# Two outlook-attention layers: the first pair's statistics pass keeps its transposed blocks in SBUF, and its stores, zero fills and output weights move into the first columns of the loop

## The chip, the cores and the metric

The kernel runs on one core of one Trainium2 chip. A core has five engines with instruction streams of their own: TensorE (PE; its weight loads are listed as PEld), VectorE (DVE), ScalarE (ACT), GpSimd (POOL) and SyncE (SP), and 16 DMA engines. Here SP and ACT issue all transfers that the kernel asks for, each on a queue of its own. The metric is the device time of one execution in microseconds, given as the median over several runs.

## The reference

The input x is 8 images of 56 x 56 positions with 384 channels, in float32. Two layers follow one another, each of the form x + f(groupnorm(x)). Group norm takes mean and variance over a whole image for each of 32 groups of 12 channels, so nothing of an image can be normalized before all of it was seen.

```python
# layer 0 (heads 12, 32 channels each), g = groupnorm(x)
v    = g @ Wv.T                                   # values, then 3x3 patches of them, zero outside
a    = softmax((g @ Wa.T).reshape(b, n, 12, 9, 9) * 32**-0.5)   # 9x9 weights per position and head
out  = einsum('bnhpq,bnqhd->bnphd', a, patches(v))
y    = overlap_add(out)                           # each of 9 results goes to its own neighbour
x    = x + y @ Wo.T
# layer 1 (heads 6, 64 channels each), g = groupnorm(x)
a    = softmax((g @ W_attn + b_attn).reshape(b, n, 6, 9))       # 9 weights per position and head
v    = g @ W_v + b_v
x    = x + einsum('bpKhd,bphK->bphd', patches(v), a) @ W_proj + b_proj
```

## The kernel before, in words

**Tiling.** The images are worked in 4 pairs. The two images of a pair lie above one another: R = 112 rows, 56 columns. The layer 0 loop goes over columns, one step for each column of each pair (4 x 56 steps and 3 more). Eight groups of 7 columns (`px`) of a pair are the patches in which attention weights meet values. All matmuls have the channels or the positions on the partitions, 128 or 112 of them.

**The opening.** Before the loop the kernel computes the group-norm statistics of pair 0, alone. It reads x in 14 blocks of 4 columns (`stats_load`, 672 KB each, into `xr`, two buffers), turns each block with 12 TensorE transposes into `xt` (channels on partitions, two buffers; three chunks of 128 channels, `stats_chunk`), copied out of PSUM by ACT, and feeds DVE's `bn_stats` from it. When a block is whole, SP stores it to the DRAM tensor `xT` (line 413). `norm_params` then adds up the statistics, spreads them over the groups by small matmuls with the matrix `gmat` (`over_groups`: for each of two quantities three output chunks of 128 channels, each summed over three input chunks) and makes scale and bias. Other work at the head of SP's and POOL's streams: loads of the weights `wv` and `wo`, zero fills of DRAM tables (`clears`, `fill`), zeroing of the two large SBUF buffers `zs` (line 455), the first of which also holds the raw weights `wa` before they are rearranged.

**The loop.** In step c `attend` projects column c of the normalized `xn` on the attention weights (lines 119, 486, 487), ACT takes exp (491), DVE sums and inverts, POOL scales (510). It also projects values (`bank<-wv_t`), which ACT copies and stores to the table `vtab0` (line 296, ACT's queue). `presum` for column c-2 adds neighbouring weights on POOL (529 to 533), and `fold` for column c-3 shifts them by a small matmul (`pw`), the result of which goes to the tables `ztab0` (line 561, ACT's queue). `upkeep` does what has to be done beside it: statistics of the next pair (loads on ACT's queue, one chunk a step), clearing, `load` of an `xT` block into `xin` (two buffers, ACT's queue, line 460), and `normed`, which turns `xin` into `xn`, with 8 columns in two halves. At column 10 of a group of seven `fetch_v` has SP read the patches of `vtab0`, one step later `fetch` has it read those of `ztab0` into the two `zs`, and the residual `xres` from `xT`. The contraction (`pc`) and the output projection (`po`, with `wo`) of the patch are queued as jobs with the due time step + 4 and are run two a step between the matmuls of the following columns.

**What sets the order.** A planner orders each engine's instructions. It starts what is ready, by its own estimate, and prefers what comes earlier in the program, so that a load can stand far ahead of its place in the code. A buffer of a pool goes to the next tile when every user of the former tile is through. `tc.keep_in_program_order` pins an instruction behind the instruction that precedes it in the program on the same engine. All matmuls and transposes and all zero fills are pinned. [...]

**Layer 1** follows with the same columns and patches, other tables and a matrix for values and weights together; the change doesn't touch it, but for `norm_params`, which makes its scale and bias too.

Of the kernel before, what the change touches and what calls it, by code (L numbers as in the profile page):

```python
# [8 lines left out]
F32 = mybir.dt.float32  # L9
# [6 lines left out]
def two_outlook_layers(  # L16
# [32 lines left out]
    nc = tc.nc  # L49

    B, H, W, C = x.shape
    P = 128
    NCH = C // P
    IMG = 2
    R = IMG * H
# [65 lines left out]
    def transpose(*args, **kwargs):  # L121
        tc.keep_in_program_order(nc.tensor.transpose(*args, **kwargs))  # L122


    ident = const.tile([P, P], F32, name="ident")
    make_identity(nc, ident)
# [49 lines left out]
    def fill(table, first, dims, width):  # L176

        src = zeros[: dims[0][1], :width]
        if len(dims) > 1:
            src = src.unsqueeze(1).to_broadcast([dims[0][1], dims[1][1], width])  # L180
        tc.keep_in_program_order(
            nc.sync.dma_start(bass.AP(table.tensor, table.offset + first, [*dims, [1, width]]), src)
        )

    def clear_v(table, sx, pad):

        line = sx * C
        part = line // 12
        fill(table, 0, [[(R + GAP) * line, NPX + 1], [part, 12 * GAP]], part)
        fill(table, GAP * line, [[line, R], [C, pad]], C)  # L190
        fill(
            table, ((NPX - 1) * (R + GAP) + GAP) * line + (sx - pad) * C,
            [[line, R], [C, pad]], C,
        )

    def clear_weights(table, line, part, sx, slot, row, first, e, ep):
        fill(table, 0, [[part, MARGIN * line // part]], part)
        fill(table, (MARGIN + R) * line, [[part, (MARGIN + 1) * line // part]], part)
        top = MARGIN * line
        fill(table, top, [[line, R]], first * row)  # L200
        fill(table, top + (first + e) * row, [[line, R], [slot, sx]], (ep - e) * row)

    def clears():

        yield 0, lambda: clear_v(vtab0, SX0, 2)

        yield 0, lambda: fill(
            ztab0[0], MARGIN * LINE0 + FIRST0 * ROW0, [[LINE0, R], [SLOT0, 2]], E0 * ROW0
        )
        for n, t in enumerate(ztab0):  # L210
            yield (1, 2 * PX, 3 * PX)[n], lambda t=t: clear_weights(
                t, LINE0, 366, SX0, SLOT0, ROW0, FIRST0, E0, EP0
            )
        yield 4 * PX, lambda: clear_v(vtab1, SX1, 1)
        for n, t in enumerate(ztab1):
            yield (5 + n) * PX, lambda t=t: clear_weights(
                t, LINE1, 350, SX1, SLOT1, ROW1, FIRST1, K, EP1
            )
# [6 lines left out]
    eps_t = const.tile([P, 1], F32, name="eps_t")  # L225
    nc.gpsimd.memset(eps_t, EPS)

    def weight(pool, src, n, name):
        t = pool.tile([P, NCH, n], F32, name=name)
        nc.sync.dma_start(t, src.rearrange("(i p) n -> p i n", p=P))  # L230
        return t

    def norm_params(st, name, params, key):

        mv = stat.tile([P, NCH, IMG, 2], F32, tag="mv", name=f"mv_{name}")

        def over_groups(src, what):
            pg = ps.tile([P, NCH, IMG], F32, tag="t", name=f"p{what}_{name}")
            for j in range(NCH):
                for i in range(NCH):  # L240
                    matmul(
                        pg[:, j, :], gmat[:, i, j * P : (j + 1) * P], src[:, i, :],
                        start=(i == 0), stop=(i == NCH - 1),
                    )
            g = stat.tile([P, NCH, IMG], F32, tag=what, name=f"{what}_{name}")
            nc.vector.tensor_copy(g, pg)
            return g

        for i in range(NCH):
            for b in range(IMG):  # L250
                nc.vector.bn_aggr(mv[:, i, b, :], st[:, i, b, :, :])
        yield
        mean = over_groups(mv[:, :, :, 0], "gmean")

        part = stat.tile([P, NCH, IMG], F32, tag="part", name=f"part_{name}")
        nc.vector.tensor_sub(part, mv[:, :, :, 0], mean)
        nc.vector.tensor_mul(part, part, part)
        nc.vector.tensor_add(part, part, mv[:, :, :, 1])
        yield
        var = over_groups(part, "gvar")  # L260
        std = stat.tile([P, NCH, IMG], F32, tag="std", name=f"std_{name}")
        nc.scalar.activation(std, var, AF.Sqrt, bias=eps_t)
        scale = const.tile([P, NCH, IMG], F32, name=f"scale_{name}")
        nc.vector.reciprocal(scale, std)
        bias = const.tile([P, NCH, IMG], F32, name=f"bias_{name}")
        nc.vector.scalar_tensor_tensor(bias, mean, -1.0, scale, ALU.mult, ALU.mult)
        params[key] = scale, bias
        yield
# [49 lines left out]
    class Jobs:  # L318


        def __init__(self):
            self.queue = []
# [30 lines left out]
    def patch_tiles(name, b):  # L353
        return patch.tile([P, NPY0, C], F32, tag="vp", name=f"vp_{name}_{b}")
# [25 lines left out]
    def layer0(late, pools):  # L380
# [5 lines left out]

        stats, st1s, params, xins, attns, pres, xrs, xts = {}, {}, {}, {}, {}, {}, {}, {}

        def stats_load(pair, blk, queue):
            nm = f"{pair}_{blk}"  # L390
            xr = io.tile([P, XB, C], F32, tag="xr", name=f"xr_{nm}")[:R]
            queue.dma_start(xr, xf[pair * R : (pair + 1) * R, blk * XB : (blk + 1) * XB, :])
            xrs[pair, blk] = xr

        def stats_chunk(pair, blk, i, alone):

            nm = f"{pair}_{blk}"
            if blk == 0 and i == 0:
                stats[pair] = stat.tile([P, NCH, IMG, NBLK, 6], F32, tag="st0", name=f"st0_{pair}")
            if i == 0:  # L400
                xts[pair, blk] = io.tile([P, NCH, XB, R], F32, tag="xt", name=f"xt_{nm}")
            xr, xt = xrs[pair, blk], xts[pair, blk]
            if alone:
                pt = bank(P, 0, XB * R).rearrange("p (m r) -> p m r", m=XB)
            else:
                pt = ps.tile([P, XB, R], F32, tag="t", name=f"pt_{nm}_{i}")
            for j in range(XB):
                transpose(pt[:, j, :], xr[:, j, i * P : (i + 1) * P], ident[:R, :R])
            nc.scalar.copy(xt[:, i], pt)
            for b in range(IMG):  # L410
                nc.vector.bn_stats(stats[pair][:, i, b, blk, :], xt[:, i, :, b * H : (b + 1) * H])
            if i == NCH - 1:
                nc.sync.dma_start(
                    xTs[pair][:, :, blk * XB * R : (blk + 1) * XB * R], xt.rearrange("p i m r -> p i (m r)")
                )
                del xrs[pair, blk], xts[pair, blk]

        stats_load(0, 0, nc.sync)
        for blk in range(NBLK):
            if blk + 1 < NBLK:  # L420
                stats_load(0, blk + 1, nc.sync)
            for i in range(NCH):
                stats_chunk(0, blk, i, True)
        for _ in norm_params(stats.pop(0), "0_0", params, 0):
            pass

# [22 lines left out]
                )  # L449
        for t in banks:  # L450
            nc.vector.memset(t[:, BANK - NP0 + NL :], 0.0)
        wv_t = weight(fixed, wv0, C, "wv0_t")
        wo_t = weight(late_w, wo0, C, "wo0_t")
        for z in zs:
            nc.gpsimd.memset(z, 0.0)

        def load(g):
            pair, blk = divmod(g, NBLK)
            xins[g] = io.tile([P, NCH, XB, R], F32, tag="xin", name=f"xin_{g}")
            nc.scalar.dma_start(  # L460
                xins[g].rearrange("p i m r -> p i (m r)"),
                xTs[pair][:, :, blk * XB * R : (blk + 1) * XB * R],
            )
# [187 lines left out]
        def upkeep(step):  # L651

            pair, c = divmod(step, W)
            while clearing and clearing[0][0] <= step:
                clearing.pop(0)[1]()
            if pair + 1 < NPAIR:
                blk, i = divmod(c - 3, NCH)
                if 0 <= c and i == 0 and blk < NBLK - 1:
                    stats_load(pair + 1, blk + 1, nc.scalar)
                if 3 <= c and blk < NBLK:  # L660
                    stats_chunk(pair + 1, blk, i, False)
                elif NBLK * NCH + 3 <= c < NBLK * NCH + 6:
                    if c == NBLK * NCH + 3:
                        making["0"] = norm_params(stats.pop(pair + 1), f"0_{pair + 1}", params, pair + 1)
                    next(making["0"])
            g, j = divmod(step + XB + 2, XB)
            if j == 0 and g < NPAIR * NBLK:
                load(g)
            g, j = divmod(step + 2, XB)
            if j == 0 and g < NPAIR * NBLK:  # L670
                normed(g)

        load(0)
        load(1)
        normed(0)
        LAG = 3
        for step in range(NPAIR * W + LAG):
# [329 lines left out]
```

## Time and profile before

| what | value |
|---|---|
| median of 6 runs | 3589.42 us (3576.93 to 3609.25) |
| profiled execution, its own time | 3576.93 us |
| its span, first to last instruction | 3575.0 us |
| granted TensorE clock, mean | 0.982 |
| PE busy | 3448.5 us, 96% |
| DVE, ACT, POOL busy | 54%, 33%, 28% |
| moved by DMA | 840.73 MB, 235 GB/s on average |
| end of the last statistics of pair 0 | 82.4 us |
| first matmul of the loop | 95.06 us |
| first patch matmul (`pc`) | 206.4 us |

The profile shows one execution. Its engine rows give busy time; a row of forty digits shows the busy tenths of forty slices of the span, about 89 us each. The chain of waits goes back from the last instruction, at each step to what released it. A group of instructions has the line of the code, the engine, the operation, the tile that it writes and those that it reads, the count, busy time and mean duration, and the idle time ahead of it with what ended it. `PEq`, `ACTq` and `SPq` are the sequencers, which issue DMAs.

### The profile page before, as it was taken

What the parts mean: (1) busy time and instruction counts of PE and PEld (TensorE: products, weight loads), DVE (VectorE), ACT (ScalarE), POOL (GpSimd) and SP (SyncE); (2) the same over time, 40 slices, a digit from 0 to 9 for tenths busy, and PEclk for the clock granted to TensorE, in tenths of its full rate; (3) what the DMA queues carried; (4) which work ended last, traced back from release to release, by engine and by line L of the source; (5) the groups of instructions that cost most, each with busy time, mean ns of one, the idle gap of its engine ahead of it and who ended that gap; (6) DMA issues with size and microseconds to landing.
All of it is one profiled execution on the core that took longest, in us unless ns stands there. A gap on an engine that the chain in (4) does not pass through costs nothing.

```text
span 3575.0 us, 72232 instructions
## 1 busy us (share of the span) xinstructions
PE 3448.5 (96%) x29078; PEld 2367.7 (66%) x29078; DVE 1917.4 (54%) x4648; ACT 1166.1 (33%) x2727; POOL 986.6 (28%) x1409
## 2 busy tenths in 40 slices
PE   4999999999999999999999999989999999999998
PEld 4667767777777677777777776755565566656555
DVE  3766676667766676666766666632322222222222
ACT  2333322333333233323322232233333433334332
POOL 2444334433443434343443444410000000000000
PEclk6999999999999999999999999999999999999999
DMA  9699988688886868887657766787888788788876
GB/s 297 202 282 297 274 271 256 227 251 260 264 284 205 272 207 279 254 256 257 221 186 226 262 200 218 236 274 180 218 215 225 208 219 215 203 224 205 226 191 160
DMA packets 692253, 840.73 MB, mean 235 GB/s; under 512 B 302222, under 2 KB 596174, under 8 KB 687822
## 3 DMA queue, kind: packets, MB, share of 16 engines
q1 hardware_dynamic: 329614, 576.00, 51.3%
q10 hardware_dynamic: 362304, 260.11, 27.0%
q8 instruction: 229, 3.75, 0.5%
q14 instruction: 106, 0.87, 0.1%
HBM read 514.32 MB, written 321.66 MB: 234 GB/s over the span
## 4 chain that ended last, share of the span: by engine, by line
PE 80%; DMA 14%; DVE 2%; ACT 1%; issue 1%; POOL 1%; ACTq 0%; SPq 0%; POOLq 0%; DVEq 0%
PE bank L119 45%; PE po L119 16%; PE pc L119 11%; DMA ztab<-wz 5%; PE pw L119 4%; DMA z<-ztab 3%; PE pt L122 2%; DMA xr<-in_x 1%; DMA lgtab<-lgt 1%; PE bank L122 1%; DMA at<-lgtab 1%; DMA vtab<-v 1%; DMA x1t<-x 1%; PE pgvar L119 0%; PE pgmean L119 0%
## 5 line engine op out<-in xcount | busy, mean ns | idle before, releaser
L119 PE MATMUL bank<-wa_t,xn 128*112 128x288 f32 x4032 | 1083.9, 408 | 2.2 <-ACT xn L471 2.2
L119 PEld LDWEIGHTS bank<-wa_t,xn 128*112 128x112 f32 x4032 | 692.1, 177 | 253.2 <-issue 31.6
L510 POOL TENSOR_TENSOR at<-at,den 112x972 f32<-112x972 f32 x224 | 504.8, 2254 | 1228.8 <-DVE den L509 1185.8
L119 PE MATMUL po<-yT,wo_t 128*128 128x448 f32 (+1 forms) x2304 | 819.5, 495 | 5.3 <-DVE x1t L621 4.8
L119 PEld LDWEIGHTS po<-yT,wo_t 128*128 128x128 f32 x2304 | 432.9, 191 | 293.8 <-issue 189.9
L119 PE MATMUL pc<-z,vp 121*32 121x49 f32 (+1 forms) x17664 | 487.3, 254 | 38.8 <-DMA z<-ztab 15.6
L119 PEld LDWEIGHTS pc<-z,vp 121*32 121x32 f32 (+1 forms) x17664 | 441.3, 131 | 116.0 <-issue 84.4
L486 DVE TENSOR_REDUCE mx<-bank 112x36 f32<-112x324 f32 x672 | 327.7, 488 | 305.9 <-PE bank L119 299.2
L119 PE MATMUL bank<-wc_t,xn 128*128 128x438 f32 x1176 | 483.4, 547 | 4.4 <-ACT xn L740 2.6
L119 PE MATMUL bank<-wv_t,xn 128*128 128x384 f32 x1176 | 418.0, 492 | 0.0
L487 DVE TENSOR_TENSOR at<-bank,mx 112x324 f32<-112x324 f32 x672 | 328.9, 489 | 21.1 <-DVE mx L486 0.5
L824 POOL TENSOR_TENSOR at<-at,den 112x378 f32<-112x378 f32 x32 | 30.2, 945 | 1114.2 <-DVE den L823 763.2
L491 ACT ACTIVATE at<-at 112x972 f32<-112x972 f32 x224 | 227.0, 1014 | 334.1 <-DVE at L487 312.0
L119 PEld LDWEIGHTS bank<-wc_t,xn 128*128 128x128 f32 x1176 | 215.2, 192 | 177.0 <-issue 162.8
L740 ACT ACTIVATE xn<-x1t,bias,scale 128x168 f32<-128x168 f32 (+4 forms) x498 | 213.8, 504 | 330.3 <-DMA x1t<-x 238.5
L119 PEld LDWEIGHTS bank<-wv_t,xn 128*128 128x128 f32 x1176 | 219.2, 190 | 139.2 <-issue 18.3
L899 DVE SCALAR_TENSOR_TENSOR x1t<-po,bo_t,x1t 128x448 f32<-128x448 f32 (+1 forms) x192 | 120.2, 626 | 329.1 <-PE po L119 329.1
L555 ACT COPY wt<-pw 112x120 f32<-112x120 f32 x224 | 58.1, 259 | 659.2 <-PE pw L119 598.0
L533 POOL TENSOR_TENSOR pre<-at,at 112x108 f32<-112x108 f32 (+1 forms) x440 | 238.5, 542 | 109.3 <-DVE wt L556 94.8
L779 DVE TENSOR_TENSOR lgt<-bank,ba_t 128x54 f32<-128x54 f32 x196 | 41.4, 211 | 412.5 <-PE bank L119 412.3
L503 DVE TENSOR_TENSOR d<-at 112x432 f32<-112x432 f32 x224 | 141.3, 631 | 194.6 <-ACT at L491 194.6
L600 ACT COPY yT<-pc 128x294 f32<-128x294 f32 x256 | 103.5, 408 | 368.1 <-PE pc L119 322.7
(81 smaller groups left out, 2842.8 us busy)
## 6 DMA issues: line engine op xcount, KB each, us to landing
z<-ztab SPq DMA_DIRECT2D x64, 2352.0 KB
vp<-vtab SPq DMA_DIRECT2D x64, 1536.0 KB
ztab<-wt ACTq DMA_DIRECT2D x336, 183.8 KB
vp<-vtab SPq DMA_DIRECT2D x64, 945.0 KB
xT<-xt SPq DMA_DIRECT2D x56, 672.0 KB
xin<-xT ACTq DMA_DIRECT2D x56, 672.0 KB
xres<-xT SPq DMA_DIRECT2D x32, 1176.0 KB
x1t<-x SPq DMA_DIRECT2D x32, 1176.0 KB
```

The lines of the kernel that those rows point to most:

```text
L119: tc.keep_in_program_order(nc.tensor.matmul(*args, **kwargs))
L122: tc.keep_in_program_order(nc.tensor.transpose(*args, **kwargs))
L486: nc.vector.tensor_reduce(mx[:, pi, :], pl.rearrange("r q a -> r a q"), AX.X, ALU.max)
L487: nc.vector.tensor_tensor(at[:, pi], pl, mx[:, pi, :].unsqueeze(1).to_broadcast([R, K2, PH]), ALU.subtract)
L491: nc.scalar.activation(at, at, AF.Exp, scale=SCALE0)
L503: nc.vector.tensor_add(d4, at[:, :, 0:4], at[:, :, 4:8])
L510: nc.gpsimd.tensor_tensor(at, at, den.unsqueeze(2).to_broadcast([R, K, K2, PH]), ALU.mult)
L533: nc.gpsimd.tensor_tensor(dst, terms[0], terms[1], ALU.add)
L555: nc.scalar.copy(mid[:, 0 : E0 : E0 - 1, :], pw[:, 0 : E0 : E0 - 1, :])
L600: nc.scalar.copy(yT[:, :, :, b, rows_of], pc.rearrange("p i n y m -> p i m (n y)"))
L740: nc.scalar.activation(to[:, i, :, rows], x1ts[g][:, i, lo - first : hi - first, rows], AF.Identity, bias=bias[:, i, b : b + 1], scale=sca ...
L899: nc.vector.scalar_tensor_tensor(res, po[:, :n], bo_t[:, j : j + 1], res, ALU.add, ALU.add)
```

## The change

It has five parts.

1. The transposed blocks of pair 0 are not stored as they come. Each of the 14 has a home in SBUF that has no other use yet: the two `xin` buffers (blocks 0 and 1), the two `xt` buffers (2 and 3), and parts of a patch buffer, of both `zs`, of `yT`, `xres` and the two `x1t` (4 to 13). They are stored to `xT` by `keep_block` from within `upkeep`, two for each of the steps 0 to 6, in the order 2, 3, ..., 13, 0, 1. Blocks 0 and 1 are not loaded again, since they are in `xin`.
2. The loads of pair 0's blocks have four buffers instead of two (two more in the other patch buffer), and three are issued ahead.
3. `wo` is loaded in step 3 instead of at the head of SP's queue, `wv` behind the fifth block load; the zeroing of `zs` moves to step 8; the clears of `vtab0` and the first `ztab0` move from steps 0 and 1 to steps 3, 4 and 5.
4. `over_groups` leaves out the products of channel chunks 0 and 2, which share no group: 7 matmuls of 9.
5. All stores to `xT`, those of later pairs too, the block loads of pair 0, and the loads of `wv` and `wo` are pinned in program order on SP.

```diff
+    class InOrder:
+        def __getattr__(self, name):
+            op = getattr(self.engine, name)
+            return lambda *args, **kwargs: tc.keep_in_program_order(op(*args, **kwargs))
...
     def clears():
-        yield 0, lambda: clear_v(vtab0, SX0, 2)
-        yield 0, lambda: fill(
+        yield 3, lambda: clear_v(vtab0, SX0, 2)
+        yield 4, lambda: fill(
             ztab0[0], MARGIN * LINE0 + FIRST0 * ROW0, [[LINE0, R], [SLOT0, 2]], E0 * ROW0
         )
         for n, t in enumerate(ztab0):
-            yield (1, 2 * PX, 3 * PX)[n], lambda t=t: clear_weights(
+            yield (5, 2 * PX, 3 * PX)[n], lambda t=t: clear_weights(
...
             for j in range(NCH):
-                for i in range(NCH):
+                near = [i for i in range(NCH) if abs(i - j) < 2]
+                for i in near:
                     matmul(
                         pg[:, j, :], gmat[:, i, j * P : (j + 1) * P], src[:, i, :],
-                        start=(i == 0), stop=(i == NCH - 1),
+                        start=(i == near[0]), stop=(i == near[-1]),
                     )
...
             if i == NCH - 1:
-                nc.sync.dma_start(
-                    xTs[pair][:, :, blk * XB * R : (blk + 1) * XB * R], xt.rearrange("p i m r -> p i (m r)")
-                )
-                del xrs[pair, blk], xts[pair, blk]
+                del xrs[pair, blk]
+                if pair:
+                    keep_block(pair, blk)
+
+        def keep_block(pair, blk):
+            tc.keep_in_program_order(
+                nc.sync.dma_start(
+                    xTs[pair][:, :, blk * XB * R : (blk + 1) * XB * R],
+                    xts.pop((pair, blk)).rearrange("p i m r -> p i (m r)"),
+                )
+            )
...
+        homes = [
+            block_tile("xin", 0, 0),
+            block_tile("xin", 0, 1),
+            block_tile("xt", 0, 2),
+            block_tile("xt", 0, 3),
+            *blocks_in(first_vp[0], 2),
+            *blocks_in(z_flat[1], 3),
+            *blocks_in(z_flat[0], 1, NCH * NA0),
+            *blocks_in(projected("first").rearrange("p i m b y -> p (i m b y)"), 1),
+            *blocks_in(late_w.tile([P, NCH, T], F32, tag="xres", name="xres_first").rearrange("p i t -> p (i t)"), 1),
+            *first_x1t,
+        ]
+        more = first_vp[1][:, : 2 * XB * C].rearrange("p (k m c) -> p k m c", k=2, m=XB)
+
+        def first_load(blk):
+            xr = more[:R, blk // 2 % 2] if blk % 2 else xr_tile(0, blk)
+            stats_load(0, blk, sync, xr)
+
+        sync = InOrder(nc.sync)
+        NXR = 4
+        for blk in range(NXR - 1):
+            first_load(blk)
         for blk in range(NBLK):
-            if blk + 1 < NBLK:
-                stats_load(0, blk + 1, nc.sync)
+            if blk + NXR - 1 < NBLK:
+                first_load(blk + NXR - 1)
             for i in range(NCH):
-                stats_chunk(0, blk, i, True)
+                stats_chunk(0, blk, i)
+            if blk == 1:
+                wv_t = weight(fixed, wv0, C, "wv0_t", sync)
...
-        wv_t = weight(fixed, wv0, C, "wv0_t")
-        wo_t = weight(late_w, wo0, C, "wo0_t")
-        for z in zs:
-            nc.gpsimd.memset(z, 0.0)
+        wo_t = late_w.tile([P, NCH, C], F32, name="wo0_t")
...
             pair, c = divmod(step, W)
+            if pair == 0:
+                for n in (2 * step, 2 * step + 1):
+                    if n < NBLK:
+                        keep_block(0, (n + 2) % NBLK)
+                if c == 3:
+                    sync.dma_start(wo_t, wo0.rearrange("(i p) n -> p i n", p=P))
+                if c == 8:
+                    for z in zs:
+                        nc.gpsimd.memset(z, 0.0)
...
             g, j = divmod(step + XB + 2, XB)
-            if j == 0 and g < NPAIR * NBLK:
+            if j == 0 and 1 < g < NPAIR * NBLK:
                 load(g)
...
-        load(0)
-        load(1)
+        xins.update({blk: homes[blk] for blk in range(2)})
         normed(0)
```

## The prediction

> **What bounds the kernel now.** I read the page first, for the engine shares and the forty slices.
>
> ```profile
> PE 3448.5 (96%) x29078; PEld 2367.7 (66%) x29078; DVE 1917.4 (54%) x4648; ACT 1166.1 (33%) x2727; POOL 986.6 (28%) x1409
> ...
> PE   4999999999999999999999999989999999999998
> ...
> DMA  9699988688886868887657766787888788788876
> ```
>
> TensorE is busy for 96% of the span. Of its 126.5 us of idle (3575.0 - 3448.5) a large part lies in the first slice, where PE shows 4 and DMA 9. Next I cut the opening into stages with the busy times of windows; columns are window, length, busy us of PE, PEld, DVE, ACT, POOL, the granted clock, the DMA share, GB/s.
>
> ```profile
> 0.00:95.00 95.00, 46.92 (x210) 40.02 (x210) 35.13 (x105) 25.64 (x48) 19.28 (x34) 0.60 0.92 298
> 95.00:120.00 25.00, 24.48 (x86) 16.32 (x87) 17.54 (x38) 9.99 (x17) 7.27 (x8) 0.90 0.86 270
> 120.00:160.00 40.00, 40.00 (x178) 29.04 (x177) 32.34 (x85) 16.66 (x32) 24.96 (x33) 1.00 0.44 120
> 160.00:215.00 55.00, 49.84 (x301) 35.08 (x299) 38.99 (x99) 16.33 (x33) 30.02 (x41) 1.00 0.99 294
> 215.00:300.00 85.00, 83.91 (x862) 60.69 (x862) 55.60 (x139) 27.75 (x58) 34.62 (x52) 0.98 0.89 272
> ```
>
> Up to 95 us, the statistics of pair 0, PE works half the time and the DMA engines are at 0.92. From there PE is nearly full, and the DMA engines have one hole, 0.44 between 120 and 160. The chain of waits from 10 to 96 us names the stall:
>
> ```profile
> by line: DMA xr<-in_x 54.1%; PE bank L122 24.1%; PE pgvar L119 4.6%; PE pgmean L119 3.7%; DVE mv L251 2.8%; issue 2.7%; DVE st L411 2.2%; PE bank L119 1.5%; ACT xt L409 1.3%; ACT xn L471 0.7%; SPq L413 0.6%; ACTq L392 0.4%; ACT std L262 0.4
> ...
> 13.79 11.93 DMA xr<-in_x
> 25.72 0.14 issue
> 25.86 2.49 PE bank L122 x12
> 28.36 7.45 DMA xr<-in_x
> ...
> 84.82 3.16 PE pgmean L119 x14
> ```
>
> One block of transposes costs 2.49 us, the wait for its x load 4 to 12 us. The loads share SP's queue and the engines with the block copies to DRAM. So the opening is bound by loads, and the loop by PE. Last, costs by group in 0 to 95 us and the waits of 85 to 300 us:
>
> ```profile
> L455 POOL MEMSET z<- 128x4704 f32 x2 | 8.0, 4020 | 4.4 <-PE pg L119 4.4
> L119 PE MATMUL pgvar<-part,gmat 128*128 128x2 f32 x18 | 4.0, 353 | 0.9 <-DVE part L258 0.9
> ```
>
> ```profile
> ACT at L491 <- DMA vtab<-v: 6.5, 1, 6.5
> PE pw L119 <- POOL pre L531: 2.9, 4, 1.3
> ```
>
> The last two lines matter below: ACT can be held by a transfer, and PE's fold sits close behind POOL.
>
> [...] here 10 us windows reach 398 and stages 294 to 301 at shares of 0.93 to 0.99, so I use what the stages show. [...]
>
> **The change part by part.**
>
> *Statistics stage: -35 us.* Removed from it: 14 block stores (14 x 672 KB = 9.6 MB), the load of wo (576 KB), all zero fills of layer 0's first tables, and the two first xin loads (1.4 MB, gone for good). Left: 14 loads of 672 KB, wa 1458 KB, wv 576 KB, together 11.7 MB; at the 301 GB/s (share 0.93) that the window 10 to 82 us has, that is 39 us, done by about 41. Three loads instead of one or two are in flight ahead of the block at work. PE still starts at 9.99 (gmat) and needs 14 x 2.47 = 34.6 us, so its floor is 44.6; both limits are near, I add 1.5 us of slip: 46. From the end of the last transposes (79.5) to the end of their statistics took 2.9 us: 49. From there (82.4) to the first wa matmul (95.06) it took 12.7 us; each of two group sums drops 4 of 18 matmuls at some 0.22 us apart (3.99 us for 18): -1.8. First wa matmul at 59.9 instead of 95.06: **-35.2**.
>
> *Group sums elsewhere: -7.* 7 more calls, 2 sums each, 4 matmuls fewer; in the loop 18 take 2.25 us (552.4 to 554.7), so 14 x 4 x 0.125 = 7.0 us, on PE, which is full there.
>
> *Stores, wo and fills move into the first columns: +6.* I count DMA busy time. Before, 0 to 95 us held 87.4 us of it, 95 to 160 held 25 x 0.86 + 40 x 0.44 = 39.1. Less the two xin loads (1.4 MB at 301 GB/s = 4.6) 122 us must fit before the stage that fetches the first patches, and the new time up to that point is 59.9 + 65 = 125. The hole is thus just filled; at 95% use it needs 128. Then come the 55 us at 0.99 as before, with no room. Before, PE stood 3.2 us for the second z there. I take 3 us more there and 3 us of ACT waits under saturation; below nothing is impossible since no traffic but the xin loads leaves, and at 85% use it is 18.
>
> *Slot of xin: 0, up to 27.* xin has two buffers, both filled with blocks 0 and 1 by the statistics. The third load (step 2 by the program, on ACT's queue) gets its buffer only when block 0's store is through, and that store is kept last but one on SP: behind 12 stores, wo, 3 + 1 + 4 fills, 13.8 MB including itself. SP begins it near 40 us; with some 1 MB done by 49, 2.6 by 60 and 200 GB/s beside ACT's traffic after that (10.2 MB, 51 us) it lands near 111. Its user is the normalization for column 8, due at 59.9 + 8 x 7.4 = 119 (7.4: 15 columns in the 111 us from 95.06 to the first patch matmul at 206.4). Three us of load and 3.4 of normalization (6 x 0.57) fit. Behind that wait on ACT stand exp, the v and wt copies and the xt copies, so DVE, POOL and PE follow within a column. If the load stands early in ACT's order (at 74.7, step 2), ACT stops until the backlog is drained at full rate, near 99, plus 3: 27 us.
>
> *Zeroing of z at column 8: +3.* 2 x 4.02 us on POOL, before hidden in the load-bound stage. POOL has a gap of 2.4 us in a column (132.2 to 134.6) and pw follows pre by about 0.9 us (132.2 to 133.1). Together they cost 8.0 - 2.4 - 0.9 = 4.7, one at a time 2 x 0.7 = 1.4.
>
> *SP's pinned order: 0.* xT stores of pairs 1 to 3 (42) are now pinned behind the instruction before them on SP, such as a z or xres fetch. The jobs are due in the same order, and PE's 299.39 of 300 us in 300 to 600 hides a store that comes late by less than two blocks (6 columns). wv and wo are used long after they land (first column's v, column 17).
>
> Sum: -35.2 - 7.0 + 6 + 3 = **-33 us**. The profiled execution took 3576.9 us, of which 3575.0 span; it is the fastest of the six, 12.5 under their median. Set against that median, 3589.4 - 33 = **3556 us**.
>
> **The rivals.**
>
> *DMA debt.* The backlog is worked off at 85% use (122 / 0.85 = 143 us) and the fetch stage runs at 0.91 (55 / 0.91 = 60): the second z lands at 203 instead of 215. Gain 12 + 7 = 19 us, the zeroing of z hidden under the wait: 3570. For: no slack in the count above. Against: 0.99 was held for 55 us.
>
> *ACT held by the slot.* As priced, 27 us lost and some 4 won back because the backlog is gone: -33 + 27 - 4 = -10: 3579. For: the load's place by the program is step 2. Against: before, xin loads stand right where their buffer falls free (96.81, 103.31, 134.73).
>
> *Slower: pinned stores.* A store of pairs 1 to 3 stands behind a waiting fetch on SP, xt's two buffers stay full, ACT's xt copy waits and exp with it. 42 stores: from 33 / 42 = 0.8 us each the gain is gone, from 1.2 us it is slower by 0.5%; at 1.6 us (67 us) the time is 3589 + 34 = 3623. For: SP's fetches did wait, up to 39 us for vtab. Against: a store has 6 columns of room.
>
> That the change does nothing would need loads that stay late with three in flight; the bytes speak against it.
>
> **How the numbers follow.** Chances: likeliest 0.55 (own range 3543 to 3567), DMA debt 0.23, ACT held 0.10, pinned stores 0.12. What this kernel's times can tell from no change is about 0.5%, 18 us: below 3571 is faster. That is the likeliest and a little over half of DMA debt: 0.68. The rest of DMA debt and ACT held: 0.20. Slower: 0.12. The range runs from a gain of 52 (opening 36.7 without slip, sums 7, the 5.7 us that PE idled between 95 and 215 gone as well, and 3 for the scatter of such medians), 3537, to 11 us past ACT held, 3590, since its 27 us is an estimate; that leaves out the slower rival and little else.
>
> **What would show it.** The first wa matmul near 60 us and xr gone from the chain's head; 14 matmuls in each pgmean and pgvar; DMA share near 0.95 with no hole up to the first z; second z landing near 182 to 188; pw waiting for pre around column 8 by 1 to 5 us. Wrong if ACT shows one long wait ahead of an xin load before 110 us, if the first pc comes after 200, or if PE falls under 99% between 300 and 1600 us.

## The result, and the profile after

The changed kernel takes 3573.01 us in the median of 16 runs (3556.9 to 3583.26), the kernel before 3588.54 in 37 runs beside them. The ratio is 0.9952, 95% interval 0.9939 to 0.9966: a gain of some 17 us (12 to 22), just inside the 0.5% that I had called the limit of a telling difference. I had forecast 33 us, and 3556.

The profiled execution of the changed kernel lies above its median (3578.47 us), the one before below its own (3576.93), so their spans, 3576.8 and 3575.0, can't be set against each other. Layer 1, of which the change touches only the group sums, took 1187.8 us in the one and 1169.3 in the other, counted from the last residual addition of layer 0 (`x1t`, which starts at 2389.0, before at 2405.7) to the end; over the thirteen profiles of this study it lies between 1161.6 and 1187.8. So I compare traces only up to the end of layer 0. When the last fold weights of the loop (`wt`) start, the changed kernel is 17.8 us ahead (2320.6 against 2338.4), as the ratio says, and 16.7 at that last addition. The page of the changed kernel, the same rows as before:

```profile
PE 3451.3 (96%) x29014; PEld 2364.1 (66%) x29014; DVE 1918.6 (54%) x4648; ACT 1165.5 (33%) x2727; POOL 987.0 (28%) x1409
...
PE   7899999999999999999999999989999999999998
...
DMA  7999988688877778887667676677778787777876
```

PE's first slice rose from 4 to 7: the opening is shorter. But the second, 9 before, is 8 now. Where that went is seen in windows of the changed kernel (columns as in the prediction):

```profile
10.00:50.00 40.00, 29.13 (x164) 26.01 (x165) 25.38 (x77) 21.60 (x41) 6.82 (x9) 0.91 1.01 304
50.00:60.00 10.00, 6.27 (x32) 5.92 (x31) 5.55 (x21) 2.60 (x4) 0.00 (x0) 0.61 1.04 396
60.00:70.00 10.00, 7.76 (x27) 5.41 (x28) 3.38 (x9) 7.27 (x14) 5.59 (x2) 0.70 0.83 283
70.00:80.00 10.00, 10.00 (x41) 6.81 (x40) 8.99 (x20) 2.40 (x3) 5.22 (x4) 1.00 0.30 86
80.00:90.00 10.00, 9.54 (x40) 6.29 (x39) 7.70 (x20) 2.74 (x5) 7.00 (x8) 1.00 0.39 139
90.00:100.00 10.00, 10.00 (x45) 7.26 (x44) 8.76 (x22) 2.80 (x6) 6.54 (x10) 1.00 0.72 211
100.00:110.00 10.00, 10.00 (x46) 7.33 (x45) 8.76 (x23) 2.33 (x5) 5.88 (x7) 1.00 0.76 214
110.00:120.00 10.00, 9.05 (x41) 6.24 (x39) 7.58 (x19) 3.89 (x7) 7.30 (x12) 1.00 1.02 331
120.00:130.00 10.00, 0.00 (x0) 0.00 (x0) 2.32 (x7) 0.00 (x0) 3.84 (x5) 0.70 0.92 296
```

Two things stand out. From 120 to 130 us PE does nothing at all. And from 70 to 90 us, where PE is full, the DMA engines run at 0.30 and 0.39, although 8 MB of the moved traffic are still to go: I had counted on 0.95 there. The stall first, as PE and then ACT with its queue show it in order of time (start, busy us, group, idle time before and what ended it):

```profile
63.02 10.40 PE L119 MATMUL bank<-wa_t,xn 128*112 128x288 f32 x36 [2.23 <-ACT xn L529]
...
132.65 5.61 PE L119 MATMUL bank<-wa_t,xn 128*112 128x288 f32 x12 [13.60 <-ACT xn L529]
```

```profile
126.70 3.74 ACTq L518 DMA_DIRECT2D xin<-xT  x2
131.56 2.90 ACT L529 ACTIVATE xn<-xin,bias,scale 128x224 f32<-128x224 f32 x6 [11.79 <-DMA xin<-xT]
```

The first `wa` matmul comes at 63.02 instead of 95.06, which the same view of the kernel before shows:

```profile
95.06 5.40 PE L119 MATMUL bank<-wa_t,xn 128*112 128x288 f32 x11 [2.18 <-ACT xn L471]
```

Column 8's comes at 132.65, 13.6 us late, since ACT stands in front of the third `xin` load until 126.70. That load waits for the store of block 0 out of the `xin` buffer, whose semaphore (107) takes its last step at 126.63. Why the store is late is in SP's queue (start, time to the end of the row's last issue):

```profile
46.85 8.63 SPq L435 DMA_DIRECT2D xT<-z  x4
55.90 2.58 SPq L132 DMA_DIRECT2D wo_t<-in_wo  x1
58.54 20.00 SPq L192 DMA_DIRECT2D vtab<-zeros  x3
85.83 0.52 SPq L435 DMA_DIRECT2D xT<-yT_first  x1
...
94.21 7.34 SPq L435 DMA_DIRECT2D xT<-x1t_first  x2
101.60 7.64 SPq L192 DMA_DIRECT2D ztab<-zeros  x4
109.29 1.81 SPq L435 DMA_DIRECT2D xT<-xt  x1
111.14 10.33 SPq L435 DMA_DIRECT2D xT<-xin  x2
```

SP begins the three fills of `vtab` at 58.54, has issued the third only at 78.5, and issues the next store at 85.83. Block 0's store goes out at 111.14; I had it *landed* at 111. What SP waited for between 60 and 112 us:

```profile
SPq L192 <- DMA vtab<-v: 13.1, 2, 6.8
SPq L192 <- DMA vtab<-zeros: 11.3, 1, 11.3
SPq L435 <- DMA vtab<-v: 7.2, 1, 7.2
SPq L435 <- DMA ztab<-wt: 6.3, 1, 6.3
SPq L192 <- DMA ztab<-zeros: 4.6, 1, 4.6
```

The columns are the time in us, the number of waits and the longest. So SP, which after the first fill went out at 60.3 us still has 8 MB to issue (6 stores of 672 KB and 3.9 MB of fills), spends most of this time waiting for single transfers of the loop (`vtab<-v`, `ztab<-wt`) and for its own fills. The trace also shows on what such a wait hangs. All 1934 transfers of SP and ACT in the changed kernel's trace name one of the same eight semaphores, counters that step up as a transfer lands. The third `vtab` fill, issued at 78.23, names number 110 and waits for 110, which had last gone to a `vtab<-v` that ACT issued at 76.15; its last step came at 78.21. From the end of the issue before, 71.90, to 78.23 SP issued nothing, and the six stores stood behind: 20.00 us for three issues, with the DMA engines at 0.30 from 70 to 80 us.

The smaller answers of the changed kernel, sums up to 96 us and the zeroing of `z`:

```profile
L119 PE MATMUL pgvar<-part,gmat x14: 343/353/353, 57.7 to 60.4; 128*128 128x2 f32 x14
```

```profile
64.41 7.98 POOL L721 MEMSET z<- 128x4704 f32 x2 [34.04 <-DMA xT<-z]
```

The sums have 14 matmuls instead of 18. The zeroing, written in step 8, was started by the planner at 64.41, as soon as the stores out of `z` were through, in a stretch in which POOL had nothing to do.

### The profile page after: what moved, and what is told of

It is laid out like the page before. It is cut to its first block, busy times and chain, and to the rows that moved or that the text cites. A ratio compares the mean times of both kernels' runs of the same rounds, so it can differ in the third digit from the quotient of the medians.

```text
span 3576.8 us, 72091 instructions
## 1 busy us (share of the span) xinstructions
PE 3451.3 (96%) x29014; PEld 2364.1 (66%) x29014; DVE 1918.6 (54%) x4648; ACT 1165.5 (33%) x2727; POOL 987.0 (28%) x1409
## 5 line engine op out<-in xcount | busy, mean ns | idle before, releaser
L119 PEld LDWEIGHTS bank<-wa_t,xn 128*112 128x112 f32 x4032 | 693.0, 177 | 270.7 <-issue 32.1
L119 PE MATMUL bank<-wc_t,xn 128*128 128x438 f32 x1176 | 492.9, 556 | 4.1 <-DMA wc_t<-in_wv 2.9
```

The source lines that it names most:

```text
L119: tc.keep_in_program_order(nc.tensor.matmul(*args, **kwargs))
```

## The experiments

Unless said otherwise an edit is to the changed kernel. "Loop" is the time from the first `mx` of column 0 to the start of the last `wt` copy of layer 0 in the one profiled execution; it is 2240.1 us before and 2254.4 after. The lines that it is read from, before and after (the times of the first and the last are what counts):

```profile
L486 DVE TENSOR_REDUCE mx<-bank x672: 424/496/499, 98.3 to 2322.8; 112x36 f32<-112x324 f32 x168
L555 ACT COPY wt<-pw x224: 236/259/274, 119.3 to 2338.4; 112x120 f32<-112x120 f32 x112
```

```profile
L544 DVE TENSOR_REDUCE mx<-bank x672: 426/496/499, 66.2 to 2305.8; 112x36 f32<-112x324 f32 x168
L613 ACT COPY wt<-pw x224: 237/259/274, 86.1 to 2320.6; 112x120 f32<-112x120 f32 x112
```

Ratios are to the kernel before on the same chip. How far a loop scatters between executions of one kernel was not measured; of the runs below, two pairs that differ in their first loads alone agree within 0.4 and 0.7 us.

**The sums alone**, in the kernel before.

```diff
-                for i in range(NCH):
+                near = [i for i in range(NCH) if abs(i - j) < 2]
+                for i in near:
...
-                        start=(i == 0), stop=(i == NCH - 1),
+                        start=(i == near[0]), stop=(i == near[-1]),
```

> The kernel before with part 4 alone: 7 products of 9 in each group sum. If matmuls saved are saved on the path (theory A, the prediction's term): 1.8 us in the opening and 7.0 in the rest, ratio 0.9975. If other waits hide them: 0.999 to 1.000.

Measured: ratio 0.9959 (0.9946 to 0.9972). The first `wa` matmul came at 92.77 instead of 95.06, and the loop took 2234.2 us, 5.9 less than before; together 8.2 us, where I had counted 1.8 + 7.0. Six of the seven later calls lie in the loop, for which the count of 0.125 us a matmul gives 6.0. The ratio says more (15 us, 10 to 19), which the trace doesn't show up to the end of layer 0; by the ratios alone the rest of the change would be worth 0.0007, which is within the noise. By the traces the rest of the change is worth -17.8 + 8.2 = -9.6 us, of which the opening gives -32.1 + 2.3 = -29.8 and the loop takes back 2254.4 - 2234.2 = **+20.2**.

**Stores in the order 0 to 13**, so that the `xin` buffers come free first.

```diff
-                        keep_block(0, (n + 2) % NBLK)
+                        keep_block(0, n)
```

> The changed kernel, but blocks 0 and 1, which sit in the two xin buffers, are stored first (order 0, 1, 2, ..., 13) instead of last. Theory A (the xin slot: the third xin load waits for block 0's store, which stands last on SP's queue): the xin load is issued before 80 us instead of at 126.7, PE's 13.6 us of idle at column 8 and the 2.5 us of slow matmuls behind it go, the first wa matmul stays near 62, the end of layer 0 comes some 16 us earlier: ratio to the kernel before 0.991. Theory B (the moved traffic as such is what costs, wherever its order): the idle time moves to the first z instead, the end of layer 0 moves by under 5 us: ratio 0.994 to 0.995.

Measured: ratio 0.9929 (0.9906 to 0.9953). ACT's wait and the 13.6 us are gone, yet the loop took 2253.2 us, 1.2 less, and ended 1.1 later; the ratio, between the two forecasts, doesn't decide. PE now waits in other places between 110 and 220 us: 6.8 us for ACT's copy of `v` and 6.8 for POOL's `pre`. The DMA share from 70 to 90 us was still 0.53 and 0.34. So the buffer decided where the lost time shows, and not how much is lost.

**Stores of pairs 1 to 3 not pinned** (42 of them).

```diff
-            tc.keep_in_program_order(
-                nc.sync.dma_start(
+            ins = nc.sync.dma_start(
...
+            if pair == 0:
+                tc.keep_in_program_order(ins)
```

> The changed kernel, with the 42 xT stores of pairs 1 to 3 not pinned in program order. Theory A (the slot costs, the pins don't): as the changed kernel within 4 us, ratio 0.995, the 13.6 us at column 8 still there. Rival (pinned stores hold ACT through xt): 10 us or more below the changed kernel, ratio 0.992 or less, with fewer waits of the xt copies.

Measured: ratio 0.9938 (0.9918 to 0.9958), and layer 0 ended 1.3 us earlier than in the changed kernel (2387.7 against 2389.0). The 10 us or more of the rival aren't there; its ratio, 0.992 or less, is at the edge of the interval, but the trace leaves the 42 pins 1 to 2 us.

**No third and fourth `xin` load**: blocks 2 and 3 stay in the two `x1t` buffers and are normalized from there; blocks 12 and 13 take the `xt` buffers.

```diff
...
-                        keep_block(0, (n + 2) % NBLK)
+                        keep_block(0, (12, 13, *range(4, 12), *range(4))[n])
...
-            if j == 0 and 1 < g < NPAIR * NBLK:
+            if j == 0 and 3 < g < NPAIR * NBLK:
...
-        xins.update({blk: homes[blk] for blk in range(2)})
+        xins.update({blk: homes[blk] for blk in range(4)})
```

> The changed kernel, with blocks 2 and 3 kept in the two x1t buffers and used from there as 0 and 1 are from xin, so that the third and fourth xin load (1.4 MB) fall away; stores in the order 12, 13, 4 to 11, 0 to 3, so the place of block 0's store in SP's queue is as late as before, but nobody needs its buffer until column 10. Theory A (slot): PE's idle time at column 8 gone, ratio 0.990 to 0.991. Theory B (moved traffic): 4.6 us of transfers fewer, so ratio 0.994, with PE idle at the first z instead. If A holds here and in the run with blocks 0 and 1 stored first, the slot is the cause and not the changed order of the stores.

Measured: ratio 0.9947 (0.9927 to 0.9968), loop 2250.0 us. Again no stall at column 8, and again it moved (10.2 us of PE waiting for `pre`); the DMA share from 70 to 90 us was 0.31 and 0.35. The 4.4 us that the loop gained are about what the 1.3 MB that are no longer read take at the 304 GB/s that the changed kernel shows from 10 to 50 us.

After these four my theory was a new one, C: the loop pays for what the DMA engines leave undone before the first patch fetches, because SP stands behind waits. Its rival, B: the moved bytes cost what they cost, wherever they stand.

**All 14 stores in column 0**, so that neither `wo` nor a fill stands between them; fills and `wo` as in the change.

```diff
-                for n in (2 * step, 2 * step + 1):
+                for n in range(NBLK) if step == 0 else ():
```

> The changed kernel with all fourteen block stores of pair 0 issued in column 0 (order 2 to 13, then 0 and 1), so that neither the output weights nor a zero fill stands between two of them; fills and weights stay at columns 3 to 5. Theory C (the opening's gain is given back because SP stands among its stores behind zero fills that wait for the loop's own small transfers, the DMA engines idle at 0.30 and 0.39 between 70 and 90 us, and the backlog meets the first patch fetches): the DMA share stays at 0.8 or more from 60 to 95 us, block 0's store has landed by about 95 us instead of about 126, ACT's wait at the load of the third xin block and PE's idle of 13.6 us at column 8 are gone, the loop of layer 0 takes 2236 to 2242 us instead of 2254, and its end lies 12 to 18 us earlier than in the changed kernel; ratio to the kernel before 0.990 to 0.992. Rival B (the moved bytes themselves cost it, wherever they stand): the idle time only moves, the loop stays at 2248 to 2254 us, ratio 0.9935 to 0.996. Rival S (only the slot of block 0): like the run with stores in the order 0 to 13, ratio about 0.993.

Measured: ratio **0.9892** (0.9870 to 0.9913), an interval that lies wholly below that of the changed kernel. Two windows of it, 70 to 110 and 110 to 220 us, and under them the same two of the changed kernel:

```profile
70.00:110.00 40.00, 39.55 (x166) 27.76 (x165) 31.94 (x75) 14.01 (x24) 23.79 (x27) 1.00 0.69 207
110.00:220.00 110.00, 95.16 (x742) 68.27 (x741) 70.53 (x180) 34.08 (x70) 48.46 (x68) 0.95 0.95 289
```

```profile
70.00:110.00 40.00, 39.54 (x166) 27.68 (x165) 34.21 (x82) 10.27 (x18) 24.64 (x28) 1.00 0.54 162
110.00:220.00 110.00, 88.93 (x710) 63.35 (x709) 60.42 (x154) 36.17 (x73) 45.72 (x66) 0.91 0.95 293
```

The DMA engines idle 12.4 us instead of 18.4 in the first window, PE 14.8 instead of 21.1 in the second, and the loop is 6.6 us shorter (2247.8). Block 0's store went out by 69 us. The same bytes in another order shortened the loop by 6.6 us, so B alone is wrong; but C missed too: the loop is still 13.6 us longer than with the sums alone, where C had 2 to 8, and it ends 4.4 us earlier than in the changed kernel, where C had 12 to 18. The ratio says more than the traces here as well: 0.006, some 21 us with an uncertainty of 9, from four executions. The hole had moved behind the stores: the share is 0.51 from 80 to 90 us, and SP now stood 22.6 us among the `vtab` fills and 13.9 among those of `ztab`.

**The fills at columns 0, 0 and 1 again**, the rest as in the change.

```diff
-        yield 3, lambda: clear_v(vtab0, SX0, 2)
+        yield 0, lambda: clear_v(vtab0, SX0, 2)
...
-        yield 4, lambda: fill(
+        yield 0, lambda: fill(
...
-            yield (5, 2 * PX, 3 * PX)[n], lambda t=t: clear_weights(
+            yield (1, 2 * PX, 3 * PX)[n], lambda t=t: clear_weights(
```

> The changed kernel with the three zero fills of tables 0 back at columns 0, 0 and 1, as before the change; the stores keep their order and columns, the output weights stay at column 3. Theory C: the fills go out before the loop's v and weight transfers exist, so they wait for none of them, and the DMA engines are busier at 70 to 90 us (0.6 or more against 0.30 and 0.39); but eight stores stand behind the first two fills and ten behind part of the third, so about half of the 16 to 20 us comes back: loop 2242 to 2248, ratio 0.992 to 0.994. Rival (the placing of the fills behind the first columns is what helps, or is of no account): ratio 0.995 to 0.998, with the loop at 2254 or longer.

Measured: ratio 0.9945 (0.9926 to 0.9964), loop 2257.1 us. I had been wrong that early fills wait for nothing of the loop. SP's longest wait in this run, and the DMA engines meanwhile:

```profile
SPq L192 <- DMA vtab<-v: 18.3, 1, 18.3
```

```profile
70.00:80.00 10.00, 10.00 (x35) 6.89 (x34) 6.46 (x15) 3.88 (x6) 0.00 (x0) 0.85 0.00 2
```

For 10 us next to nothing moves, share 0.00 and 2 GB/s, while ten of the fourteen block stores have yet to be issued. It is the plainest sight of the mechanism: a queue with work, idle engines, and one transfer at its head that waits.

**The first two x loads in the two plain buffers**, the next two in the borrowed ones.

```diff
-            xr = more[:R, blk // 2 % 2] if blk % 2 else xr_tile(0, blk)
+            xr = more[:R, blk % 2] if blk // 2 % 2 else xr_tile(0, blk)
```

> The changed kernel with the first two x loads in the two plain load buffers and the third and fourth in the borrowed ones; nothing else. If the 2 to 5 us by which the opening missed the forecast (first column at 66.2 us by the trace, where 98.3 - 35.2 = 63.1 was forecast) come from the second load, which waits until 9.44 us for memory of the setup: first column at 62 to 64 us, DMA share of 0 to 10 us at 0.5 or more instead of 0.32. Theory C expects most of that to be given back in the loop (ratio 0.994 to 0.996); the rival, that what the opening gains stays gained, 0.994 less 0.0008: 0.993 to 0.9945.

Measured: ratio 0.9944 (0.9927 to 0.9962), first `wa` matmul at 60.47 instead of 63.02, loop 2254.8. In the changed kernel the second load is issued only at 9.44 us, since it goes into memory that the setup uses; here both go out by 1.7 us, and the two loads into that memory from 9.42. Of these 2.5 us 2.1 stayed gained in the trace up to the end of the loop (2318.5 against 2320.6); theory C had expected most of it to be given back, and was wrong in that. The ratios can't tell it.

**This with all stores in column 0, in the order 0 to 13.**

> As the run with all stores in column 0, with the stores in the order 0 to 13 besides, and with the first two x loads going into the two plain load buffers, so that the second load need not wait until 9.4 us for memory that the setup uses. Theory C: loads start some 5 us earlier, the first column starts 2 to 5 us earlier than 66 to 68 us, the rest as in that run: ratio 0.988 to 0.991. Rival B: the earlier start is given back as well, ratio 0.993 to 0.996, with the loop longer by what the start is earlier.

Measured: ratio 0.9908 (0.9891 to 0.9926), loop 2248.2 us, layer 0 over at 2380.5. Start earlier by 4.4 us than in the run with the stores first (64.0 against 68.4), end by 4.0; so the earlier start stayed gained here too. Two things were changed at once, so what the order of the stores does alone isn't shown by it.

**Everything of pair 0 in column 0**: stores, then `wo`, then the fills.

```diff
-                for n in (2 * step, 2 * step + 1):
+                for n in range(NBLK) if step == 0 else ():
...
-                if c == 3:
+                if c == 0:
                     sync.dma_start(wo_t, wo0.rearrange("(i p) n -> p i n", p=P))
```

(with the fills at columns 0, 0, 0.)

> As the run with all block stores in column 0, and the output weights and the zero fills of tables 0 in column 0 too, behind the stores: the same bytes as there, but no transfer of pair 0 that SP still has to issue stands at columns 3 to 5, where it waited for the loop's transfers (22.6 us in front of the second and third v fill, 13.9 us among the weight fills). In that run the loop of layer 0 took 2247.8 us and the DMA engines were at 0.51, 0.80 and 0.51 from 80 to 110 us. Theory C (SP standing behind waits is the whole of what the loop still loses against the 2234.2 us of the run with the sums alone): DMA share 0.85 or more until 100 us, the idle time of TensorE between 120 and 200 us falls from about 15 us to 5, loop 2236 to 2240, ratio 0.985 to 0.988. Rival B (the bytes that now move beside the loop, 9.4 MB of blocks, cost what is left): loop 2245 to 2250, ratio 0.989 to 0.991, the idle time only moved.

Measured: ratio 0.9908 (0.9888 to 0.9928), loop 2243.7 us, between the two forecasts and 10.7 us shorter than the changed kernel's with the same bytes. The edit didn't do what it was for. In SP's queue, in order of time:

```profile
68.36 1.28 SPq L132 DMA_DIRECT2D wo_t<-in_wo  x1
71.77 22.80 SPq L192 DMA_DIRECT2D vtab<-zeros  x3
95.30 15.56 SPq L192 DMA_DIRECT2D ztab<-zeros  x4
```

```profile
SPq L192 <- DMA xin<-xT: 27.4, 2, 20.0
```

The fills take as long as when they stood at column 3, and the longest wait (20.0 us) ended with `xin<-xT`, a load on ACT's queue. I had taken it that this load waited for its block's store, and the next expectation but one says so. The trace doesn't bear it out: the semaphores of the stores of blocks 0 and 1 are full at 75.3 and 77.4 us, and the load goes out at 87.78, where it stands in ACT's order. The fill and the load name the same counter, 103. Writing the fills earlier didn't free them from a counter that a late transfer held, here for 20.0 us. Why the loop is nonetheless 4.1 us shorter than with the stores first isn't shown.

**This with the two early loads**, by the edit shown above.

> The same with the first two x loads in the two plain load buffers, so that the opening begins 2 to 5 us earlier (first column 63.7 us instead of 66.2 in the run with that edit alone). Theory C: 2 to 4 us faster than the run without it, ratio 0.984 to 0.987; rival B: the same as without it, within 1 us, the loop longer by what the start is earlier.

Measured: ratio 0.9893 (0.9870 to 0.9915), loop 2243.0 us, start 3.0 us earlier, end of the loop 3.7 earlier (2307.3 against 2311.0).

**This without the third and fourth `xin` load** (the edit shown above, on top), so that no `xin` load stands on ACT's queue in that stage.

> The run with everything of pair 0 issued in column 0 and the two early loads, and besides blocks 2 and 3 are kept in the two x1t buffers and normalised from there, so that ACT loads no xin block from DRAM before column 20 or so and 1.3 MB less is read. In the run without this edit SP stood 20 us in front of a v fill because a completion counter was still held by one of those xin loads, which itself waited for its block's store; the DMA engines idled for 13.2 us between 70 and 110 us and the loop took 2243.0 us. Theory C (idle DMA engines ahead of the first patch fetches are what the loop pays for): the idle DMA time from 70 to 110 us falls to 8 us or less, and the loop to 2236 to 2240 us, ratio 0.986 to 0.988. Rival B (what is left is the price of the moved bytes themselves): loop 2242 to 2246 us, ratio 0.989 to 0.991, even if the idle DMA time falls.

Measured: ratio 0.9884 (0.9858 to 0.9909), loop 2236.9 us. The two windows, and under them the second one of the kernel before:

```profile
70.00:110.00 40.00, 38.53 (x158) 26.10 (x157) 32.56 (x79) 12.14 (x23) 25.59 (x29) 1.00 0.73 218
110.00:220.00 110.00, 104.85 (x790) 74.35 (x789) 79.18 (x199) 37.69 (x75) 54.29 (x78) 1.00 0.99 302
```

```profile
110.00:220.00 110.00, 103.74 (x614) 73.87 (x613) 81.96 (x205) 37.23 (x73) 63.98 (x86) 0.98 0.77 227
```

PE idles 5.2 us from 110 to 220 (6.3 before the change, at a DMA share of 0.77, now 0.99), and the loop is within 2.7 us of the 2234.2 with the sums alone. Layer 0 ends at 2369.3, 36.4 us ahead of the kernel before, where I had forecast 33 for the change, which has none of these edits. SP still stands 15.1 us among the `vtab` fills, now behind `vtab<-v` (13.8 us the longest). Idle DMA time fell less than C had said (10.8 us, not 8 or less), and the 1.3 MB that are read no more are worth some 4.5 us by themselves, by an estimate from the 302 GB/s of the second window. So this run shows that the opening's gain can be kept, and leaves open how much of its last 6 us is the shorter wait and how much the fewer bytes.

All runs with the stores moved in one table, single executions; idle times are window length less PE busy, and window length times one less the DMA share:

| kernel | DMA idle 70-110 | PE idle 110-220 | loop | its end |
|---|---|---|---|---|
| fills early | 18.4 | 19.0 | 2257.1 | 2327.4 |
| early loads | 16.0 | 22.3 | 2254.8 | 2318.5 |
| changed kernel | 18.4 | 21.1 | 2254.4 | 2320.6 |
| stores 0 to 13 | 15.6 | 13.7 | 2253.2 | 2321.7 |
| not pinned | 19.6 | 20.7 | 2250.7 | 2318.6 |
| no reload | 19.6 | 15.3 | 2250.0 | 2318.1 |
| stores first, early loads | 14.0 | 11.0 | 2248.2 | 2312.2 |
| stores first | 12.4 | 14.8 | 2247.8 | 2316.2 |
| all in column 0 | 12.4 | 11.2 | 2243.7 | 2311.0 |
| the same, early loads | 13.2 | 12.3 | 2243.0 | 2307.3 |
| the same, no reload | 10.8 | 5.2 | 2236.9 | 2300.7 |

The six kernels that leave the DMA engines idle for over 15 us take 2250 to 2257, the five under 15 take 2237 to 2248. But these five are also all that have the stores in column 0, and within the six the kernels with the most idle time have the shortest loops. So the idle time goes with the loss, and that it makes the loss is argued. What is shown is the order: with everything in column 0 the same bytes cost 10.7 us less of the 20.2. The other 9.5 remain open; the last two edits take 6.8 of them, 1.3 MB of reads included.

The five best ratios, 0.9884 to 0.9908, all belong to kernels with the stores first, and their intervals overlap: each of them is about 1% faster than the kernel before, and which is best isn't settled.

## Why the prediction was half right

*Statistics stage, -35.2: right in kind, 32.0 in size.* The first `wa` matmul moved from 95.06 to 63.02. The last transposes ended at 50.6, not 46: the second load left only at 9.44 us (worth 2.5 us, by the run with the early loads), and PE still waited 1 to 2 us for a load ahead of several blocks; 12.4 us instead of 13.8 then passed to the first `wa` matmul.

*Group sums, -7.0 and -1.8: right*, 5.9 (six of the seven calls) and 2.3 measured.

*Zeroing of z, +3: wrong, and nothing.* I took the code's step for the place in time. The planner had POOL do it at 64.41, when it was idle; PE's waits for `pre` from 110 to 200 us sum to 1.5 us, and no zeroing stands beside them.

*SP's pinned order, 0: right for pairs 1 to 3*, by the run without those pins. For pair 0 it is where the loss sits, and I hadn't thought of it there; no run took pair 0's pins away, so whether they or the place of the fills in the program are to blame is open.

*Stores, wo and fills, +6, and the slot of xin, 0: this is the step that failed.* Together with the zeroing I had 9 us for what the loop gives back; it was 20.2. The sum of busy DMA time was sound: up to the first `z` fetch it was 154 us before (0.82 of 188.2) and 146 after (0.84 of 174.2), where the 4.6 us of `xin` loads make 150. The 95% use that I put on it was not. From 66.2 to 110 us the share was 0.54, as SP stood in front of transfers that wait for others. I treated SP's queue as a pile that the DMA engines empty at their own pace, though the prediction itself shows ACT held for 6.5 us by a transfer. The slot followed from the same error: the store that should have landed near 111 was issued at 111.14, and the load behind it at 126.70. That stall of 13.6 us was conspicuous, and still only the form of the loss, as the runs with no stall there showed. In its place the runs show a queue that couldn't issue: SP took 20.00 us for three fills. The order on that queue is shown to be 10.7 of the 20.2 us; the rest is open.

*The rivals.* The measured 3573 lies outside the 3543 to 3567 of the likeliest case. The nearest rival is the DMA debt: gain 19, second `z` landed at 203; the wait for it ended at 201.66. It gave 3570, and its reason, a backlog worked off at low use, is what the traces show. That its figure is so close is in part luck: it had 85% up to 143 us, where the trace has 0.90 up to 60, 0.54 from 66 to 110 and 0.95 from there to 220. ACT held by the slot was seen where I said (a wait of over 10 us ahead of an `xin` load), later than I said.

*What would show it.* Right: 14 matmuls in each sum, the first `pc` before 200 (192.8), PE at 99.4% and more from 300 to 1600 us. Wrong: DMA share without a hole, second `z` between 182 and 188.

## What to carry to other kernels

Bytes divided by a rate say how long a backlog takes only if the queue can issue it: I counted on a share of 0.95, and from 66 to 110 us the trace has 0.54. Where an order on a queue is pinned, put the transfers that wait for nothing ahead of those that wait (here the loop was 6.6 us shorter with all stores in column 0), and for each transfer ask whose completion releases it: a buffer (block 0's, whose store went out at 111.14 and let the load behind it go at 126.70), a table (a patch fetch of the kernel before waited up to 39.0 us for `vtab<-v`), or a counter that some transfer of another queue holds (20.0 us with everything in column 0). When removing a visible stall doesn't shorten the stage (13.6 us gone, the loop 1.2 us shorter), look one resource further back, for engines that idle while there is work for them, here the DMA engines 40 us earlier, at 0.30 and 0.39.

## What the runs showed that I had not expected

The stall at column 8 cost more than its length. After 13.6 us without work the 12 `wa` matmuls of column 8 took 5.61 us, against 3.15 for the same twelve at 81.59 us in the same run, so 2.5 us more. PE's last matmul ended at 119.05; the granted clock was 1.00 from 119 to 124 us and 0.50 from 124 to 137.6. And the first zero fill of `vtab`, 445 KB, held the next fill of the same table for 11.3 us, from 60.3 to 71.6, since both name the same counter, 108. It took one step at 60.39 and none from there to 68.49, while transfers that SP had issued before it landed (the counters of three stores out of `z` are full at 62.6, 64.3 and 66.0, that of `wo` at 67.5); its last step came at 71.55. The next fill, 336 KB, landed 2.7 us after its issue. The first one's counter got nine single steps at the end, from 68.49 to 71.55, and the next one's sixteen, from 73.78 to 74.29; what that has to do with the time was not tried.
